# Two Mamba-style layers in one kernel: B of two states by diagonal matrices, the skip product D*u moved from TensorE to VectorE, and some smaller edits of order and layout

## The chip, the core and the metric

The kernel runs on one core of a Trainium2 chip. The metric is device time in microseconds of one execution; a kernel's time is the median of its runs. In the profile, PE is TensorE (PEld its weight loads), DVE is VectorE, ACT is ScalarE, POOL is GpSimd and SP is SyncE, which here issues nearly all DMAs. Each engine works through its own queue in order.

## The reference

The input is 8 images of 48 x 48 pixels with 192 channels. Two layers follow each other, each with a residual, each fed by a group norm. Both expand to 384 inner channels and run a selective scan with 16 states. Cut to what matters:

```python
# layer 0: four directions k of an image (rows, columns, both also backwards)
xi, z = split(einsum('bhwc,oc->bhwo', x, in_proj_w)); z = silu(z)
xi = silu(conv3x3_depthwise(xi) + conv_b)
x_dbl = einsum('bkdl,kcd->bkcl', xs, x_proj_w)          # per k: 12 dt ranks, B (16), C (16)
dt = softplus(einsum('bkrl,kdr->bkdl', dts, dt_w) + dt_bias)
h = exp(dt*A) * h + (dt*u) * B;  y = sum_n(h * C)        # the scan over 2304 pixels
y = sum of the four directions of (y + Ds*xs)
y = layernorm(y) * ln_w + ln_b
x = x + einsum('bhwd,od->bhwo', y * z, out_proj_w)
# layer 1: two stages (down the columns, then along the rows), each the sum of a forward
# and a backward Mamba over lines of 48 pixels
xs = silu(causal_conv_3taps(xs) + conv_b)
y = selective_scan(xs, dt, B, C, A) + xs * D
out = einsum('nld,cd->nlc', y * silu(z), out_proj_w)
```

## The kernel before

**Tiling.** The work is cut into items of 384 pixels: 8 lines of 48. Each layer has 192 items (layer 0: 8 images x 4 directions x 6 chunks; layer 1: 2 stages x 8 images x 6 chunks x 2 directions). The 384 channels lie as 3 blocks (`j`) of 128 partitions. An item has 16 states and so 48 segments, one for each state and block. A segment is one scan of 128 x 384 on VectorE.

**The path of one segment.** `stream` runs these as lanes:
- `decays` (L426, ACT): exp(dt*A) into a tile of the pool `a` (layer 0, 12 of them) or of `das` (layer 1, 16).
- `weighs` (L450 on POOL for the whole state, or L455 on ACT in three activations): `bT`, which is dt*u with pixels on the partitions (`dtu`, three blocks of 128 pixels x 384 channels), times B, a scalar per partition.
- `places` (L474, PE): transposes the three blocks of `bT` into a PSUM tile `b`, which gives dt*u*B with channels on the partitions. There are three such PSUM banks. State 8 alone is *direct*: B itself is transposed and VectorE multiplies by dt*u (L485).
- `scans` (L1234, L994, DVE): the scan, from `a` and `b` into `h`. Layer 0 carries the last column of `h` into the next item (L969, POOL copies it to `carry`).
- `gathers` (L509, POOL): `h` times C for the three blocks of a state; C comes broadcast by DMA as `cc` (`fetches`).
- `adds` (L526, PE): transposes `h` back and sums over the states in three PSUM banks `y`. In layer 1 nine matmuls per item with diag(D) (L538, `l_diag`) add D*u into the same banks.
- `leave` (L571): copies `y` out and transposes it back into a work bank `yb_ps`; `finish` takes it from there on VectorE (L1005, L1009 in layer 0: adds into `acc`; L1238 in layer 1: multiplies the gate `z`).

Ahead of the segments, `project` makes x_dbl of a pair of items (L295, `xd_ps`), copies it out, transposes B (`bt`) and makes dt (L338). `products` multiplies dt by u on POOL (L366) and transposes it into `dtu`. Softplus, silu and exp lie in different tables of ScalarE, so softplus and silu are done for several tiles at once and the table of exp is then put back (`tables`, L212). In layer 0, `enters` does one block of three silu thirds of `u` per image and one softplus block per pair; `prologues` computes the next image's input projection and convolution in the background; `tails` does the layer norm, the gate (silu of `z`, loaded from DRAM) and the output projection of a chunk after its fourth direction. Layer 1 has `inputs`, `gates`, `begins` and `output` for the same purposes. All work matmuls share two PSUM banks.

**The order.** The order in which the program emits instructions is the order of the queues. Each layer has a `Plan`: every step is a `Need` with a due time in segments, a cost for each engine that could do it, the steps it must come after, and whether it takes or frees a work bank. `Plan.run` simulates the engines with these costs and emits, at each point, the step that can start first, and among those ready the one due first; steps with several engines (bT on POOL or ACT, copies on ACT or DVE) go where they start first. So costs and due times set every queue's order, DMA queue included, and how bT is shared.

```python
yield Need(s + 6, {PE: 0.22}, sets=done)                  # L537: one D*u product
costs = {ACT: 0.51}; ... costs[POOL] = 2.07               # weighs: one block on ACT, a whole state on POOL
Need(need.due + 1, {DVE: 0.45}, [need], frees=need.bank, sets=[mark("gated", i, j)])   # layer 1's gate
```

Of the kernel before, what the change touches and what calls it, by code (L numbers as in the profile page):

```python
# [13 lines left out]
ALU = mybir.AluOpType  # L14
# [22 lines left out]
DIRECT = ((8,), (8,))  # L37
PE, DVE, ACT, POOL, SP = "PE", "DVE", "ACT", "POOL", "SP"
# [142 lines left out]
class Common:  # L181
# [54 lines left out]
    def diagonals(self, out, w):  # L236

        for i in range(w.shape[1]):
            self.nc.vector.tensor_scalar(out[:, i, :], self.ident, w[:, i : i + 1], None, ALU.mult)

# [38 lines left out]
    def project(self, plan, pool, p, pair, lo, mid, hi):  # L279
# [3 lines left out]

        nc, mark = self.nc, plan.mark
        tiles = {}
        dts, evacs = [], []
        for i, item in enumerate(pair):
            g, wts = 2 * p + i, item["wts"]
            at = pace(mid if i else lo, hi if i else mid, 12)
            for j in range(NJ):  # L290
                n = Need(at(), {PE: item["cost"][0]}, item["ready"] if j == 0 else (), bank=(j == 0))
                yield n
                if j == 0:
                    ps, k = self.bank(n, "xd_ps"), n.bank
                nc.tensor.matmul(  # L295
                    rows(ps[:E, :T]), wts["xp"][:, j, :], item["u"](j),
                    start=(j == 0), stop=(j == NJ - 1),
                )
# [3 lines left out]
            self.copy(got.e, xd, ps[:E, :T])  # L302
# [53 lines left out]
    def products(self, plan, pool, items, direct):  # L356

        nc, mark = self.nc, plan.mark
        last = max(n for n in range(N) if n not in direct)
        for g, item in enumerate(items):  # L360
            after = [mark("dt", g)] + ([mark("multiplied", g - 2), mark("turned", g - 2)] if g >= 2 else [])
            n = Need(g * NSEG - 20, {POOL: item["cost"][1]}, after, sets=[mark("du", g)])
# [4 lines left out]
            for b in range(TB):  # L367
                at = g * NSEG - 13 + 2 * b
# [13 lines left out]
                after = [n] + ([mark("bT", g - 2, last, b) for b in range(TB)] if g >= 2 else [])  # L382
                plan.then(Need(at + 1, COPY, after, frees=n.bank, sets=[mark("dtu", g, b)]), out)
# [9 lines left out]
    def stream(self, plan, pool, items, direct, decay, scan, finish, held, kept, weighed):  # L393
# [14 lines left out]
        states = [n for n in range(N) if n not in direct]  # L408
# [49 lines left out]

        def places():
            for s in range(total):  # L460
# [3 lines left out]
                after = [mark("bt", i)] if n in direct else [mark("bT", i, n, b) for b in range(TB)]  # L464
                if s >= 3:
                    after.append(mark("scan", s - 3))
                yield Need(s - 1.5, {PE: 0.33}, after, sets=[mark("place", s)])
                bps[s] = ps = self.ps_b.tile([P, 512], F32, tag="b", name="b")
                for b in range(TB):
                    if n in direct:  # L470
# [26 lines left out]
        def gathers():  # L497

            for f in range(total // NJ):
# [3 lines left out]
                if "carry" in item:  # L503
                    yield Need(NJ * f + 2.5, {POOL: 0.15}, after, sets=[mark("carry", i, n)])
                    item["carry"](n, hs[f])
# [5 lines left out]
        def adds():  # L511
            for s in range(total):
# [20 lines left out]
                if "diag" in item and 10 <= r < 10 + NJ * TB:  # L533

                    j, b = divmod(r - 10, TB)
                    done = [mark("skipped", i)] if r == 9 + NJ * TB else ()
                    yield Need(s + 6, {PE: 0.22}, sets=done)  # L537
                    nc.tensor.matmul(  # L538
                        item["sum"][b][:, j * P : (j + 1) * P],
                        item["own"][:, j, b * P : (b + 1) * P], item["diag"][:, j, :],  # L540
                        start=False, stop=False, skip_group_check=True,
                    )
# [33 lines left out]
        for lane in (fetches, decays, weighs, places, scans, gathers, adds):  # L576
            plan.start(lane())
        plan.start(self.products(plan, pool, items, direct))
# [3 lines left out]
def layer0(ctx, cm, x, xs, x2, w, norm):  # L582
# [36 lines left out]
    def piece(b, c, due, tag="xc", bufs=3, after=(), of=x):  # L619
# [19 lines left out]
    def weights(b, due, after):  # L639
# [8 lines left out]
        for c in range(NC):  # L648
            xc, n = yield from piece(b, c, due, after=ends[-3:-2])
# [63 lines left out]
    def gate_inputs(b, wb, ready, lo, hi):  # L713
# [3 lines left out]
        for c in range(NC):  # L717
            xc, got = yield from piece(b, c, at(), after=ends[-3:-2])
# [27 lines left out]
    def prologues():  # L746

        after = yield from first()
        for b in range(1, NIMG):
# [4 lines left out]
            for j in range(NJ):  # L754
                diag, made = yield from matrices(j, at(), conv)
                pads = []
                for c in range(NC):
                    xc, got = yield from piece(b, c, at(), after=ends[-3:-2])
# [17 lines left out]
    def first():  # L776
# [8 lines left out]
        def pads_of(c):  # L785
            nonlocal ends
            xc, got = yield from piece(0, c, -95, after=ends[-3:-2])
# [47 lines left out]

    def enters():

        for p in range(len(items) // 2):
# [3 lines left out]
            if q < 3:  # L842
# [8 lines left out]
                yield Need(lo, {ACT: 2.05 + 2 * TABLE}, after, sets=[mark("u", b, q)])  # L851
                part = slice(q * L // 3, (q + 1) * L // 3)
                nc.scalar.activation(u[:, :, part], u[:, :, part], AF.Silu)
                cm.tables()
            pair = items[g : g + 2]
            after = yield from cm.project(plan, pool, p, pair, lo, mid, hi)
            yield Need(hi, {ACT: 2 * 1.07 + 2 * TABLE}, after, sets=[mark("dt", g), mark("dt", g + 1)])
            cm.softplus(pair)
            cm.tables()

    def tails():
# [4 lines left out]
        for b in range(NIMG):  # L866
            st = None
            for c in range(NC - 1, -1, -1):
# [18 lines left out]
                n = Need(at(), {ACT: 1.06}, [n] + used)  # L887
                yield n
                sq = pool.tile([P, NJ, T], F32, tag="z", name="sq", bufs=1)
                nc.scalar.activation(sq, a, AF.Square)  # L890
                for j in range(NJ):
                    n = Need(at(), {PE: MM}, [n], bank=(j == 0))
                    yield n
                    if j == 0:
                        ps, k = cm.bank(n, "var_ps"), n.bank
# [472 lines left out]
```

## Time and profile before

| what | value |
|---|---|
| median of 3 runs | 21360.33 us (21356.79 to 21372.65) |
| the profiled execution's own time | 21367.72 us |
| its span, first to last instruction | 21366.0 us |
| granted clock of TensorE | 0.991 |
| busy: PE, DVE, ACT, POOL | 20418.5, 19769.0, 20367.7, 20007.4 us (96, 93, 95, 94% of the span) |
| weight loads (PEld) | 15817.8 us (74%) |
| DMA | 1512 MB, mean 71 GB/s |
| first scan of layer 0, last of layer 0 | 104.3 us, 10778.7 us (starts) |
| first scan of layer 1 | 10902.4 us (start) |

Busy time of an engine is the union of its instructions' lengths. Instructions of one engine overlap at their ends, so a group's busy time can hold some time in which the next one was already running; the distance from one start to the next is the finer measure of what an instruction takes from its engine. The lines are those of the kernel before.

### The profile page before, as it was taken

To read this page: it belongs to the slowest core of one execution; us is meant where nothing else is said; L and a number is where in the kernel's file an instruction comes from. 1 tells how busy PE (TensorE), PEld (TensorE's weight loads), DVE (VectorE), ACT (ScalarE), POOL (GpSimd) and SP (SyncE) were. 2 spreads that over 40 slices of the span, in tenths; PEclk is the share of its full clock that TensorE was granted. 3 is DMA by queue.
4 is the path that set the end of the run, shared out by engine and by line. 5 is a ranking of instruction groups with operands and counts; after the bars stand their busy time and mean duration, and the time that the engine had idled before them with its cause. 6 is when DMAs were issued, how large, how long until landed. Compare 5 with 4: busy or idle time off the path is not lost.

```text
span 21366.0 us, 391510 instructions
## 1 busy us (share of the span) xinstructions
PE 20418.5 (96%) x138640; PEld 15817.8 (74%) x138640; DVE 19769.0 (93%) x24601; ACT 20367.7 (95%) x38324; POOL 20007.4 (94%) x10538
## 2 busy tenths in 40 slices
PE   9989999899999999988889999999999999999999
PEld 6767777676776777766667777777777777777777
DVE  8999999999999999999979999999999999999999
ACT  8999999999999999999989999999999999999999
POOL 7999999999999999999979999999999999999999
PEclk9999999999999999999999999999999999999999
DMA  2222222222222222222222222222222222222222
GB/s 78 76 83 71 77 78 75 85 71 80 75 75 85 71 77 79 76 75 62 65 61 65 65 65 65 65 65 65 64 66 66 67 68 67 67 67 68 67 67 65
DMA packets 728904, 1512.34 MB, mean 71 GB/s; under 512 B 181508, under 2 KB 324484, under 8 KB 726824
## 3 DMA queue, kind: packets, MB, share of 16 engines
q1 hardware_dynamic: 724768, 1485.21, 23.0%
q8 instruction: 1106, 18.12, 0.4%
q14 instruction: 846, 6.93, 0.1%
q10 hardware_dynamic: 2184, 2.08, 0.0%
HBM read 1382.03 MB, written 104.99 MB: 70 GB/s over the span
## 4 chain that ended last, share of the span: by engine, by line
PE 39%; DVE 6%; ACT 4%; POOL 2%; issue 1%; DMA 0%; POOLq 0%; DVEq 0%; ACTq 0%; SPq 0%
PE b L474 12%; PE y L526 12%; DVE h L1234 3%; PE o_ps L1266 3%; PE z_ps L1171 2%; PE xi_ps L1121 2%; PE dt_ps L338 2%; PE xd_ps L295 2%; POOL h L509 2%; ACT l_da L426 1%; ACT bT L455 1%; PE y L538 1%; DVE u L1146 1%; PE du_ps L373 1%; PE yb_ps L571 1%
## 5 line engine op out<-in xcount | busy, mean ns | idle before, releaser
L509 POOL TENSOR_TENSOR h<-h,cc 128x1152 f32<-128x1152 f32 x6144 | 16158.4, 2643 | 839.7 <-DVE h L1234 205.1
L1234 DVE TENSOR_TENSOR_SCAN h<-l_da,b 128x384 f32<-128x384 f32 x9216 | 8160.5, 935 | 441.3 <-PE b L474 337.8
L474 PE MATMUL b<-ident,bT 128*128 128x128 f32 x51840 | 8022.7, 277 | 434.7 <-DVE h L994 320.8
L526 PE MATMUL y<-ident,h 128*128 128x128 f32 x55296 | 7931.6, 276 | 252.5 <-POOL h L509 235.2
L455 ACT ACTIVATE bT<-dtu,bt 128x384 f32<-128x384 f32 x14070 | 8053.2, 606 | 71.6 <-PE b L474 63.8
L474 PEld LDWEIGHTS b<-ident,bT 128*128 128x128 f32 x51840 | 6005.4, 142 | 2371.2 <-issue 721.1
L994 DVE TENSOR_TENSOR_SCAN h<-a,carry,b 128x384 f32<-128x384 f32 x7680 | 7212.0, 995 | 518.0 <-PE b L474 215.4
L526 PEld LDWEIGHTS y<-ident,h 128*128 128x128 f32 x55296 | 6363.9, 142 | 1746.7 <-POOL h L509 788.3
L426 ACT ACTIVATE a<-dt,l_A 128x384 f32<-128x384 f32 x9216 | 5206.5, 606 | 30.6 <-DVE h L994 28.2
L426 ACT ACTIVATE l_da<-dt,l_A 128x376 f32<-128x376 f32 x9216 | 5098.8, 600 | 56.6 <-DVE h L1234 53.0
L450 POOL TENSOR_TENSOR bT<-dtu,bt 128x1152 f32<-128x1152 f32 x1070 | 2264.8, 2120 | 59.0 <-PE b L474 41.5
L994 DVE TENSOR_TENSOR_SCAN h<-a,b 128x384 f32<-128x384 f32 x1536 | 1357.7, 935 | 131.2 <-PE b L474 82.5
L366 POOL TENSOR_TENSOR du<-dt,u 128x1152 f32<-128x1152 f32 x384 | 1074.8, 2799 | 166.5 <-ACT dt L354 149.1
L295 PE MATMUL xd_ps<-u,l_xp 128*44 128x384 f32 x2304 | 1143.1, 586 | 5.2 <-ACT u L1140 2.6
L338 PE MATMUL dt_ps<-xd,l_dtw 12*128 12x384 f32 x2304 | 1045.1, 535 | 0.5 <-ACT dtu L220 0.5
L738 PE MATMUL cv_ps<-pad,diag 128*128 128x384 f32 x2376 | 950.9, 489 | 1.2 <-DVE acc L1009 0.9
L1171 PE MATMUL z_ps<-xt,l_z 96*128 96x384 f32 x2304 | 922.0, 491 | 23.5 <-DVE u L1146 22.5
L1266 PE MATMUL o_ps<-z,l_out 128*96 128x384 f32 x2304 | 930.5, 486 | 0.0
L1121 PE MATMUL xi_ps<-xt,l_u 96*128 96x384 f32 x2304 | 845.5, 496 | 54.4 <-DVE u L1146 41.9
L969 POOL COPY carry<-h 128x3 f32<-128x3 f32 x2560 | 507.2, 198 | 247.4 <-DVE h L994 221.1
L1146 DVE SCALAR_TENSOR_TENSOR u<-xi_ps,l_conv_w,u 128x376 f32<-128x376 f32 (+1 forms) x1152 | 685.9, 595 | 53.0 <-ACT u L1140 27.6
L485 DVE TENSOR_TENSOR b<-b,du 128x384 f32<-128x384 f32 x1152 | 629.7, 547 | 81.2 <-PE b L474 80.9
(123 smaller groups left out, 14278.8 us busy)
## 6 DMA issues: line engine op xcount, KB each, us to landing
cc<-bc SPq DMA_DIRECT2D x3072, 384.0 KB, 3.5
xc<-in_x SPq DMA_DIRECT2D x186, 288.0 KB, 4.4
z<-v SPq DMA_DIRECT2D x144, 192.0 KB, 1.9
z<-z SPq DMA_DIRECT2D x48, 576.0 KB, 4.3
v<-v SPq DMA_DIRECT2D x126, 192.0 KB, 2.0
u<-v SPq DMA_DIRECT2D x21, 1152.0 KB, 8.0
xc<-in_xs SPq DMA_DIRECT2D x48, 288.0 KB, 3.5
x<-xc SPq DMA_DIRECT2D x48, 288.0 KB, 3.0
```

The source lines that it names most:

```text
L295: nc.tensor.matmul(rows(ps[:E, :T]), wts["xp"][:, j, :], item["u"](j), start=(j == 0), stop=(j == NJ - 1),)
L338: nc.tensor.matmul(ps[:, :T], wts["dtw"][:, j * P : (j + 1) * P], xd[:R, :], start=True, stop=True)
L426: nc.scalar.activation(dst, src, AF.Exp, scale=item["A"][:, j, n : n + 1])
L450: nc.gpsimd.tensor_tensor(to, of, by.to_broadcast((P, TB, DI)), ALU.mult)
L455: nc.scalar.activation(to[:, b, :], of[:, b, :], AF.Copy, scale=by[:, b, :])
L474: nc.tensor.transpose(ps[:, b * P : (b + 1) * P], of, self.ident)
L509: nc.gpsimd.tensor_tensor(h, h, c, ALU.mult)
L526: nc.tensor.matmul(item["sum"][b][:, j * P : (j + 1) * P], hs[f][:, j, b * P : (b + 1) * P], self.ident, is_transpose=True, skip_group_che ...
L994: nc.vector.tensor_tensor_scan(order(h[:, at % NJ, :]), order(a), order(b[:, :T]), carry[:, at : at + 1] if item["carried"] else 0.0, ALU. ...
L1171: nc.tensor.matmul(pieces(ps), wz[d][0][:, m, j * P : (j + 1) * P], lines(xts[p % 3], m, d), start=(m == 0), stop=(m == NM - 1),)
L1234: nc.vector.tensor_tensor_scan(h[:, at % NJ, :], a, b[:, :T], 0.0, ALU.mult, ALU.add)
L1266: nc.tensor.matmul(ps[:CP, :T], wout[:, 2 * stage + e, j, m * CP : (m + 1) * CP], items[2 * p + e]["z"][:, j, :], start=(e == 0 and j == 0 ...
```

## The change

For layer 0:
- **Column x products in image order.** For the two column directions, x_dbl is computed with the pixels in the order of the image (rows of 8 pixels) and turned into column order by the copy out of PSUM. The additions into `acc` for these directions run in image order as well, reading `yb_ps` at a stride.
- **1/sigma in PSUM.** The squares are made in three parts; Ln and Exp of the variance stay in the PSUM bank, and the multiplication by 1/sigma reads them there.
- **Joined table loads.** Thirds 1 and 2 of the next image's silu, and the silu of `z` for the items that have ended, are done in the softplus block of a pair (`block`). `z` has two tiles and is loaded before that block.
- **Two states by diagonal B.** States 4 and 11 get no bT. A lane `matrices` makes diag(B) for the three pixel blocks, on POOL in one instruction or on ACT in three, and `places` multiplies dtu by it: nine fp32 matmuls per state in place of nine transposes.
- Buffers: `a` has 9 tiles instead of 12, `xc` two instead of three.

For layer 1:
- **D*u by VectorE.** The nine L538 matmuls per item and `l_diag` go. `finish` adds u*D to `y` in PSUM by one `scalar_tensor_tensor` for each block, ahead of the product with the gate. `u` has six tiles instead of five and is freed at the gate.
- **The first pair sooner.** Inputs, projections and dt*u of the first pair get due times 300 segments earlier.

```diff
+DIAGONAL = ((4, 11), ())
@@ project
+            across = (lambda v: v.rearrange("p (h w) -> p h w", w=RT)) if turned else rows
-                    rows(ps[:E, :T]), wts["xp"][:, j, :], item["u"](j),
+                    across(ps[:E, :T]), wts["xp"][:, j, :], item["u"](j),
...
+                self.copy(got.e, xd.rearrange("p (w h) -> p w h", h=S),
+                    ps[:E, :T].rearrange("p (h w) -> p w h", w=RT))
@@ stream
+        def matrices():
+            for i, item in enumerate(items):
+                for n in sorted(diagonal):
+                    after = [mark("bt", i)]
+                    if placed:
+                        after += [mark("place", placed[-1] + j) for j in range(NJ)]
+                    need = Need(i * NSEG + NJ * n - 6, {POOL: 0.8, ACT: 0.72}, after, sets=[mark("matrix", i, n)])
+                    yield need
+                    to = dbs[i, n] = pool.tile([P, TB, P], F32, tag="db", name="db", bufs=1)
+                    by = item["bt"][:, :, R + n : R + n + 1]
+                    if need.e == POOL:
+                        of = self.ident.unsqueeze(1).to_broadcast((P, TB, P))
+                        nc.gpsimd.tensor_tensor(to, of, by.to_broadcast((P, TB, P)), ALU.mult)
+                    else:
+                        for b in range(TB):
+                            nc.scalar.activation(to[:, b, :], self.ident, AF.Copy, scale=by[:, b, :])
...
-                after = [mark("bt", i)] if n in direct else [mark("bT", i, n, b) for b in range(TB)]
+                if n in diagonal:
+                    after = [mark("matrix", i, n)] + [mark("dtu", i, b) for b in range(TB)]
...
-                yield Need(s - 1.5, {PE: 0.33}, after, sets=[mark("place", s)])
+                yield Need(s - 1.5, {PE: 0.67 if n in diagonal else 0.33}, after, sets=[mark("place", s)])
...
+                        nc.tensor.matmul(
+                            ps[:, b * P : (b + 1) * P], item["dtu"][:, b, j * P : (j + 1) * P],
+                            dbs[i, n][:, b, :], start=True, stop=True)
@@ adds
-                if "diag" in item and 10 <= r < 10 + NJ * TB:
-                    yield Need(s + 6, {PE: 0.22}, sets=done)
-                    nc.tensor.matmul(item["sum"][b][:, j * P : (j + 1) * P],
-                        item["own"][:, j, b * P : (b + 1) * P], item["diag"][:, j, :], ...
@@ layer0, enters
-                yield Need(lo, {ACT: 2.05 + 2 * TABLE}, after, sets=[mark("u", b, q)])
+                if q == 0 or b == 0:
+                    yield from block(lo, after, thirds=[(b, q)])
+                thirds = [(b, q + 1)] if q < 2 and b else []
+            ended = [g - 2, g - 1] if p and (g - 2) % per >= 3 * NC else []
+            for i in ended:
+                n = Need(hi - 20, {SP: 0.1}, [mark("z used", gated[-2])] if len(gated) > 1 else [], lag=DMA)
...
+                yield from block(hi, after, pair, thirds, ended)
+    def block(due, after, pair=(), thirds=(), ended=()):
+        tables = 1 + bool(pair) + bool(thirds or ended)
@@ layer0, tails
-                rs = sq[:, 0, :]
-                nc.scalar.activation(rs, ps[:, :T], AF.Ln, bias=eps)
+                rs = ps[:, :T]
+                nc.scalar.activation(rs, rs, AF.Ln, bias=eps)
                 nc.scalar.activation(rs, rs, AF.Exp, scale=-0.5)
@@ layer0
-        return pool.tile([P, T], F32, tag="a", name="a", bufs=12), lambda a, dt: (a, dt)
+        return pool.tile([P, T], F32, tag="a", name="a", bufs=9), lambda a, dt: (a, dt)
-            a, yj = seen(acc, j, k, c), rows(y)
+            a, yj = by_rows(seen(acc, j, k, c), k), by_rows(rows(y), k)
@@ layer1
+    NU = 6
+    SOON = 300
+            if p == 0:
+                lo, hi = lo - SOON, hi - SOON
-                        if i >= 5:
-                            after.append(mark("skipped", i - 5))
+                        if i >= NU:
+                            after += [mark("gated", i - NU, b) for b in range(NJ)]
@@ layer1, finish
+            nc.vector.scalar_tensor_tensor(
+                y, item["own"][:, j, :], item["D"][:, j : j + 1], y, ALU.mult, ALU.add)
             nc.vector.tensor_tensor(item["z"][:, j, :], item["z"][:, j, :], y, ALU.mult)
-        plan.then(Need(need.due + 1, {DVE: 0.45}, ...
+        plan.then(Need(need.due + 1, {DVE: 0.96}, ...
```

## The prediction

> **What bounds the kernel now.** I read the busy time by stretch first, because the two layers are separate programs with different limits: 2000 to 9000 us lies wholly in layer 0, 12000 to 20000 us in layer 1.
>
> ```profile
> core 0: us, PE busy (x) PEld busy (x) DVE busy (x) ACT busy (x) POOL busy (x), PEclk, DMA share, GB/s
> 2000.00:9000.00 7000.00, 6554.70 (x43918) 4985.44 (x43917) 6496.53 (x7659) 6692.15 (x12656) 6695.80 (x4357) 0.99 0.25 77
> 12000.00:20000.00 8000.00, 7929.34 (x55034) 6294.76 (x55032) 7525.18 (x9839) 7751.18 (x14542) 7513.42 (x2981) 1.00 0.22 66
> ```
>
> Everything is at 93% or more, so shares alone decide nothing; DMA (22 to 25%) and the clock (0.99) are out. An item has 48 decays: 6062 in the first stretch are 126.3 items of 55.4 us, 7052 in the second 146.9 items of 54.5 us. Next, the waits, for layer 0 (POOL) and then for layer 1 (POOL, DVE, PE):
>
> ```profile
> POOL carry L969 <- DVE h L994: 114.8, 124, 3.1
> POOL h L509 <- DVE h L994: 30.1, 34, 3.0
> ...
> POOL h L509 <- DVE h L1234: 152.8, 232, 3.6
> ...
> DVE h L1234 <- PE b L474: 263.2, 597, 1.5
> ...
> PE xi_ps L1121 <- DVE u L1146: 28.3, 49, 0.7
> PE z_ps L1171 <- DVE u L1146: 21.8, 35, 0.6
> ```
>
> In layer 0 all POOL waits together are 165 of 7000 us: POOL runs end to end and sets the pace, with ACT (95.6%) as its partner in making bT. In layer 1 POOL waits for about 475 us of 8000, the scans wait 263 us for PE's b, and PE's matmuls wait only 62 us in all. There PE sets the pace. Then the groups, out of the answers for the two stretches (us busy, mean ns):
>
> ```profile
> L509 POOL TENSOR_TENSOR h<-h,cc 128x1152 f32<-128x1152 f32 x2022 | 5344.6, 2648 | 172.0 <-DVE h L994 30.1 <-POOL h L509 5.2 <-POOL carry L969 0.2
> L455 ACT ACTIVATE bT<-dtu,bt 128x384 f32<-128x384 f32 x4815 | 2765.4, 606 | 24.0 <-PE b L474 21.6 <-PE y L526 0.4
> L450 POOL TENSOR_TENSOR bT<-dtu,bt 128x1152 f32<-128x1152 f32 x289 | 615.1, 2128 | 2.6 <-PE b L474 2.1 <-ACT dtu L220 0.5
> L1009 DVE TENSOR_TENSOR acc<-acc,yb_ps 128x384 f32<-128x384 f32 x288 | 210.2, 735 | 3.2 <-PE yb_ps L571 3.0
> L906 DVE TENSOR_TENSOR acc<-acc,sq 128x1152 f32<-128x1152 f32 x30 | 87.2, 2906 | 0.0
> L634 POOL TENSOR_TENSOR diag<-ident,l_conv_w 128x128 f32<-128x128 f32 x144 | 54.0, 408 | 0.0
> L1005 DVE SCALAR_TENSOR_TENSOR acc<-u,l_dsum,yb_ps 128x384 f32<-128x384 f32 x90 | 52.6, 589 | 1.4 <-PE yb_ps L571 1.3
> L884 DVE TENSOR_TENSOR acc<-acc,mu_ps 128x1152 f32<-128x1152 f32 x30 | 40.4, 1345 | 3.4 <-PE mu_ps L881 3.1
> ...
> L538 PE MATMUL y<-l_diag,u 128*128 128x128 f32 x2646 | 512.9, 276 | 0.0
> ```
>
> L455 and L450 give the split of the 15 bT states of an item: 12.7 on ACT, 2.3 on POOL. In order of time, TensorE shows what a D*u product costs it, start to start:
>
> ```profile
> 14015.36 0.39 PE L538 MATMUL y<-l_diag,u 128*128 128x128 f32 x2
> 14015.59 0.49 PE L526 MATMUL y<-ident,h 128*128 128x128 f32 x3
> 14015.91 0.49 PE L474 MATMUL b<-ident,bT 128*128 128x128 f32 x3
> ```
>
> 0.23 us for a product, 0.11 for a transpose (three in 0.33): the shown lengths (0.39, 0.49) hold a drain that the next instruction overlaps.
>
> **Layer 0, diagonal states.** Two bT states per item go. On ACT one is three activations spaced 0.51 us apart (seven decays in 3.65 us), 1.5 us; on POOL it is 2.1 us. Each gets a diag(B) instead, 128x384. POOL bounds: 0.41 us for 128 columns (L634), 2.13 for 1152 with the same broadcast (L450), so 0.83 by the line between. ACT: three of the 0.26 us of the bt copy (128x132), 0.8. I take 0.8. The planner in the kernel shares bT by its own costs (0.51, 2.07), which agree with the trace, so I count all of it on ACT and then rebalance: ACT loses 2 x (1.5 - 0.8) = 1.4 us per item. PE gains 18 products for 18 transposes: 18 x 0.12 = +2.1 us. The matrix has one buffer and its place waits for it and for all three dtu blocks; behind it in PE's queue stand adds and work matmuls. Three b banks cover about 3 us; without that cover a late matrix costs up to 0.8 us, twice per item.
>
> **Layer 0, table loads.** Silu of thirds 1 and 2, and of the gate, joins the softplus blocks. Before: 2 loads each for 24 thirds, 96 pairs, 48 gates = 336. After: 6 + 14 (first thirds) + 192 (pairs) + 30 (a third table where something joined) + 2 = 244. 92 x 1.29 us = -119 us on ACT, 0.6 per item. Squares in three parts: +0.35 us x 48, 0.1 per item. The joined block holds ACT up to 8.3 us (three tables 3.9, two softplus 2.3, silu 2.1), while decays in stock fall from 12 to 9: 9 x 1.15 = 10.4 us of scans, enough but with little over; some 30 such blocks could cost 0 to 2 us each.
>
> **Layer 0, rebalanced.** ACT falls by 1.4 + 0.6 - 0.1 = 1.9 us. Moving d states from POOL to ACT until both fall alike: 2.1 d = 1.9 - 1.5 d, d = 0.53, so both fall 1.1 us. POOL, which sets the pace, gives 1.1 to 1.15 us per item. I take 1.15: L906 at 2.9 us runs beside a busy POOL, the last one, with POOL idle, took 1.36, so POOL too should stall less. 192 x 1.15 = **-221 us** (bounds 0.4 and 1.5: -77 to -288).
>
> **Layer 0, what costs nothing or helps beside it.** Column xd products took 1.40 us start to start (3105.34 to 3106.74) against 0.77 in image order: -0.63 x 3 on half the items = -0.95 on PE, which pays half of the diagonals' 2.1. L906 with 1/sigma in PSUM should cost L884's 1.35: -1.6 us x 48 on DVE. Odd acc additions (0.85 us each in a column pass) should cost 0.53: -0.32 x 288 on DVE. Against this last speaks the Trainium skill, SBUF — State Buffer, section Door 1: PSUM has 8-byte lines and a non-contiguous PSUM pattern slows matmuls significantly; yb_ps is now read at a stride of 48 elements. The row that does that today, the 96x384 addition of o_ps (L945), takes 537 ns against 538 for a straight copy, so I take 0.53; were the rule right for DVE, this saving would be 0, and the sum the same, as DVE (92.8%) is not the pace. The z loads leave the tail: same 48 transfers of 576 KB, but issued on SP before the block, past the cc fetches, instead of waiting for L906 at the head of SP's queue. SP has room.
>
> **Layer 1, D*u.** PE loses 9 x 0.23 = 2.0 us per item; DVE gains three operations of L1005's form, 0.51 (spacing) to 0.59: 1.5 to 1.8 us, ahead of the gate product; scans queue behind it, and the work bank stays taken 0.5 us longer. The eased u buffers (six, freed at the gate) come free about when five did. Now the sum of three engines: DVE 51.2 + ACT 52.8 + POOL 51.1 = 155.1 us per item, +1.7 = 156.8, mean 52.3 if copies and bT are shared out again. At layer 0's mean use (94.7%) that gives 55.2 us, slower by 0.7; at ACT's use in layer 1 (96.9%) 54.0; if PE alone counted, 52.5. Rule against row: the Trainium skill, Perfetto Trace Analysis, Identifying the Most-Contended Engine, holds matmul occupancy a bad measure and wants weight-load occupancy, here 6295 of 8000 us, 79%. By it PE has room, ACT is the most contended, and this edit brings nothing or a loss. By the waits PE is the pace and up to 2.0 us come out. I side with the waits but let the three others stop it early: -0.55 us, 53.9. 192 x 0.55 = **-106 us** (bounds -1.3 and +0.4: -250 to +77).
>
> **Between the layers.** Last scan of layer 0 ends about 10779.7, first of layer 1 starts at 10902.41. From the first pair's normalised xt (10824.9) to that scan are 77.5 us, in which PE alternates xd and dt with z and the next pair's xi. The pair alone needs, by the same rows: xi and taps to 10841.9, silu 3.5, xd 4.3, copy and dt about 8, softplus with tables 4.8, du 2.6, dtu 0.6, bT 2.1, place 0.5: some 45 us. 32 us sooner, of which the z and xi work pushed behind it takes part back: -25. The last tail no longer waits for z and two tables (10802.1 to 10807.0): -5. Together **-30** (-5 to -50). At the start two xc buffers instead of three hold up six statistics pieces of about 3.5 us: **+5** (0 to 10).
>
> **Sum.** -221 - 106 - 30 + 5 = -352 us on the profiled execution's own 21367.7, so 21016; the runs' median lies 7 us below that execution: **21010 us**.
>
> **Rivals.**
> *Layer 1 follows PE* (14%): -2.0 x 192 = -384, with the rest 20730. For: PE's 62 us of waits. Against: ACT at 97%.
> *Layer 1 stands still* (16%): DVE, ACT and POOL keep 54.5 us; -246 us, 21115. For: their sum grows.
> *PE takes over in layer 0* (10%): in a diagonal state places and adds need 3 x (0.68 + 0.33) = 3.0 of 3.45 us, besides background matmuls; if b comes late there, layer 0 gives 60 us: 21170. Against: two states of 16, three banks.
> *D*u lands on the scan chain* (6%), the slower side: DVE's present idle time stays, and each item of layer 1 grows by the whole 1.75 us: +336 - 246 = +90, 21450. It decides from 1.5 us per item on. Against: most of that idle time is waiting for PE.
> *The plan gives it back* (4%): its new order leaves POOL as full as now and the gains elsewhere wait for it: 0 us, 21360, the unchanged time.
> My own case has 50%, its range 20880 to 21140.
>
> **How the numbers follow.** Leaving out the slower case, the unchanged one and the outer part of the first rival gives 20780 to 21230. 0.2% is 43 us, about what this measurement can tell. Faster 0.90, same 0.04, slower 0.06.
>
> **What would show it.** Right: layer 0 items near 54.3 us, POOL's bT below 2.3 per item, table loads 92 fewer, L906's successor near 1.35, column xd products at 0.8 per pair; layer 1 items near 53.9 with PE's waits grown and DVE waiting less for b; first scan of layer 1 about 90 us after the last of layer 0. Wrong: POOL waits in layer 0 grown to over 5% (PE or decays late), or DVE in layer 1 over 97% busy with items at 54.5 or more.

## The result, and the profile after

The changed kernel takes 21021.72 us (median of 4 runs, 21017.24 to 21027.79) against 21361.95 us before on the same chip: 0.984 of it, 95% interval 0.9823 to 0.9857. The profiled execution took 21021.07 us, its span is 21019.3 us, its clock 0.996. The prediction says 21010 us, 12 us from the median. That it comes so close is luck in part: layer 0 gave 48 us more than was said and layer 1 54 us less, as the scan starts in the two traces show (us; layer 0 has 192 items, layer 1 too):

| stage | before | after | difference | predicted |
|---|---|---|---|---|
| to the first scan | 104.3 | 109.0 | +4.7 | +5 |
| layer 0, first scan to last | 10674.4 | 10405.6 | -268.8 | -221 |
| last scan of layer 0 to first of layer 1 | 123.7 | 94.1 | -29.6 | -30 |
| layer 1, stage 1 | 5222.1 | 5215.9 | -6.2 | -53 |
| layer 1, stage 2 | 5219.0 | 5173.0 | -46.0 | -53 |
| after the last scan | 22.5 | 21.6 | -0.9 | 0 |

An item fell from 55.6 to 54.2 us in layer 0 and from 54.4 to 54.1 us in layer 1. The busy time of the two stretches, as shown of before:

```profile
core 0: us, PE busy (x) PEld busy (x) DVE busy (x) ACT busy (x) POOL busy (x), PEclk, DMA share, GB/s
2000.00:9000.00 7000.00, 6732.94 (x47284) 5345.49 (x47284) 6539.38 (x7802) 6703.55 (x13085) 6719.10 (x4410) 0.99 0.25 79
12000.00:20000.00 8000.00, 7828.10 (x52699) 5994.81 (x52699) 7742.41 (x10240) 7750.08 (x14599) 7640.58 (x3033) 1.00 0.22 67
```

In layer 0 POOL's share has hardly moved (95.7% to 96.0%), since the stretch holds more items (129.2, 126.3 before): per item its busy time fell from 53.0 to 52.0 us, and ACT's from 53.0 to 51.9. In layer 1 PE has gone from 99.1% to 97.9% and DVE from 94.1% to 96.8%. The waits of the changed kernel (us in total, times, longest), POOL, DVE (for both kinds of place) and ACT in layer 0, then POOL, DVE and PE in layer 1:

```profile
POOL carry L1030 <- DVE h L1059: 64.7, 75, 3.4
POOL h L548 <- DVE h L1059: 43.6, 28, 13.0
DVE h L1059 <- PE b L512: 181.2, 327, 4.5
DVE h L1059 <- PE b L503: 39.7, 76, 2.5
ACT a L435 <- DVE h L1059: 97.8, 209, 3.4
...
POOL h L548 <- DVE h L1298: 202.2, 266, 3.8
DVE h L1298 <- PE b L512: 118.3, 272, 1.3
PE b L512 <- DVE h L1298: 86.5, 304, 1.0
```

Two rows of the kernel before to set beside them, DVE in layer 0 and PE in layer 1:

```profile
DVE h L994 <- PE b L474: 172.9, 282, 3.6
...
PE b L474 <- DVE h L1234: 10.3, 46, 2.4
```

POOL still waits for almost nothing in layer 0: 1.5% at these two rows. In layer 1 the picture has turned. The scans waited 263 us for PE's transposes and now wait 118; PE waited 10.3 us for the scans to free a `b` bank and now waits 86.5. POOL waits for the scans 202 us, 50 more than before. DVE is now what the others wait for, and its own waits, all together, fell most: from 394 to 180 us, while POOL's fell from 474 to 354 and PE's rose from 62 to 153.

The granted clock of TensorE differs too (0.991 over the span before, 0.996 after), and almost all of that lies in layer 0. By the clock record of the traces, half the clock was granted for 297 us between its first and last scan before, and for 133 us after, mostly in stretches of 3.4 to 10 us. In the 3.4 us ahead of such a stretch PE was busy 46% of the time before and 56% after, against 93 and 95% on the whole, so these stretches come where PE had been waiting. What they add to the time was not separated from the waits.

The groups that the prediction's steps rest on, layer 0 and below the gap layer 1 (us busy, mean ns, then idle time before them):

```profile
L464 ACT ACTIVATE bT<-dtu,bt 128x384 f32<-128x384 f32 x4316 | 2507.7, 606 | 11.5 <-PE b L512 8.9
L459 POOL TENSOR_TENSOR bT<-dtu,bt 128x1152 f32<-128x1152 f32 x241 | 510.5, 2118 | 7.8 <-PE b L512 6.3 <-PE y L565 1.4
L483 ACT ACTIVATE db<-ident,bt 128x128 f32<-128x128 f32 x714 | 232.3, 391 | 3.2 <-PE b L503 3.0
L295 PE MATMUL xd_ps<-u,l_xp 128*44 128x384 f32 x774 | 326.3, 508 | 0.1
L1074 DVE TENSOR_TENSOR acc<-acc,yb_ps 128x384 f32<-128x384 f32 x300 | 157.3, 530 | 3.1 <-PE yb_ps L600 2.7
L971 ACT ACTIVATE acc<-acc,l_ln_b,l_ln_w 128x384 f32<-128x384 f32 x90 | 62.2, 699 | 3.5 <-DVE acc L967 3.4
L967 DVE TENSOR_TENSOR acc<-acc,var_ps 128x1152 f32<-128x1152 f32 x30 | 40.1, 1335 | 2.6 <-ACT var_ps L964 2.3
...
L1302 DVE SCALAR_TENSOR_TENSOR yb_ps<-u,l_D,yb_ps 128x384 f32<-128x384 f32 x441 | 263.7, 598 | 1.2 <-ACT l_da L435 0.8 <-ACT bT L464 0.4
```

The 7000 us hold 129.2 items: 11.1 bT states of an item on ACT and 1.87 on POOL, where it was 12.7 and 2.3. The addition L1074 takes 530 ns (735 before; both are means over straight and strided ones), the product with 1/sigma (L967) 1335 instead of 2906. One place and one matrix in order of time:

```profile
3015.80 0.83 PE L503 MATMUL b<-db,dtu 128*128 128x128 f32 x6
...
3016.47 0.49 PE L565 MATMUL y<-ident,h 128*128 128x128 f32 x3
...
3017.15 0.97 ACT L483 ACTIVATE db<-ident,bt 128x128 f32<-128x128 f32 x3
...
3017.83 0.19 POOL L1030 COPY carry<-h 128x3 f32<-128x3 f32 x1
...
3018.03 1.28 ACT L435 ACTIVATE a<-dt,l_A 128x384 f32<-128x384 f32 x2
...
3018.11 2.65 POOL L548 TENSOR_TENSOR h<-h,cc 128x1152 f32<-128x1152 f32 x1
```

Start to start, a diagonal place takes PE 0.67 us (twice a place of three transposes), the matrix takes ACT 0.88, and a carry copy takes POOL 0.28, though its own length reads 0.19. The plan of the changed kernel reckons 0.72 for that matrix and 0.15 for that copy.

### The profile page after: what moved, and what is told of

Its sections match the earlier page's. It is cut to its first block, busy times and chain, and to the rows that moved or that the text cites. A ratio compares the mean times of both kernels' runs of the same rounds, so it can differ in the third digit from the quotient of the medians.

```text
span 21019.3 us, 391720 instructions
## 1 busy us (share of the span) xinstructions
PE 20233.5 (96%) x138640; PEld 15731.1 (75%) x138640; DVE 19835.8 (94%) x25014; ACT 20092.6 (96%) x38482; POOL 19933.6 (95%) x10537
## 4 chain that ended last, share of the span: by engine, by line
PE 57%; DVE 17%; ACT 10%; POOL 9%; issue 6%; DMA 1%; DVEq 0%; POOLq 0%; SPq 0%; ACTq 0%
PE y L565 18%; PE b L512 17%; DVE h L1298 9%; POOL h L548 7%; PE dt_ps L344 4%; ACT bT L464 3%; DVE h L1059 3%; PE xd_ps L295 3%; PE cv_ps L767 3%; PE b L503 2%; PE o_ps L1333 2%; ACT l_da L435 2%; ACT a L435 2%; PE xi_ps L1190 2%; PE z_ps L1240 2%
## 5 line engine op out<-in xcount | busy, mean ns | idle before, releaser
L565 PE MATMUL y<-ident,h 128*128 128x128 f32 x55296 | 7673.2, 275 | 188.9 <-POOL h L548 175.3
L512 PE MATMUL b<-ident,bT 128*128 128x128 f32 x48384 | 7402.7, 276 | 339.2 <-DVE h L1059 162.9
L464 ACT ACTIVATE bT<-dtu,bt 128x384 f32<-128x384 f32 x13026 | 7518.3, 606 | 54.9 <-PE b L512 45.5
L565 PEld LDWEIGHTS y<-ident,h 128*128 128x128 f32 x55296 | 6273.8, 141 | 1621.5 <-POOL h L548 708.2
L512 PEld LDWEIGHTS b<-ident,bT 128*128 128x128 f32 x48384 | 5557.4, 141 | 2022.0 <-issue 629.0
L435 ACT ACTIVATE a<-dt,l_A 128x384 f32<-128x384 f32 x9216 | 5282.5, 607 | 166.3 <-DVE h L1059 152.8
L459 POOL TENSOR_TENSOR bT<-dtu,bt 128x1152 f32<-128x1152 f32 x1034 | 2188.4, 2118 | 43.8 <-PE b L512 34.0
L295 PE MATMUL xd_ps<-u,l_xp 128*44 128x384 f32 x2304 | 959.2, 505 | 21.9 <-DVE z L1305 13.9
L503 PE MATMUL b<-db,dtu 128*128 128x128 f32 x6912 | 925.1, 279 | 10.0 <-DVE h L1059 9.3
L503 PEld LDWEIGHTS b<-db,dtu 128*128 128x128 f32 x6912 | 850.7, 193 | 83.7 <-DVE h L1059 42.4
```

What stands on the lines that cost most here:

```text
L295: nc.tensor.matmul(across(ps[:E, :T]), wts["xp"][:, j, :], item["u"](j), start=(j == 0), stop=(j == NJ - 1),)
L435: nc.scalar.activation(dst, src, AF.Exp, scale=item["A"][:, j, n : n + 1])
L459: nc.gpsimd.tensor_tensor(to, of, by.to_broadcast((P, TB, DI)), ALU.mult)
L464: nc.scalar.activation(to[:, b, :], of[:, b, :], AF.Copy, scale=by[:, b, :])
L503: nc.tensor.matmul(ps[:, b * P : (b + 1) * P], item["dtu"][:, b, j * P : (j + 1) * P], dbs[i, n][:, b, :], start=True, stop=True,)
L512: nc.tensor.transpose(ps[:, b * P : (b + 1) * P], of, self.ident)
```

## The experiments

All times are medians; the changed kernel is "after" (21022). Stages are read from scan starts in each profiled execution, as above. Layer 0 of three runs below in which nothing of layer 0 was edited took 10393 to 10396 us against 10406 in after, so differences of layer 0 under about 15 us are not interpreted. Layer 1 is steadier: 10388 to 10393 us in after and the seven runs that edit nothing of it. The intervals of the ratios are about 0.0015 to each side (some 32 us), so for differences of 50 to 66 us the intervals of the two kernels still touch; what speaks for them is that the four runs of each kernel lie within 25 us, and that the kernel before took 21356 to 21363 us (medians) on the chips used.

**Layer 0: the diagonals undone.** The two states get bT again; all else stays.

```diff
-DIAGONAL = ((4, 11), ())
+DIAGONAL = ((), ())
```

> The changed kernel without the diagonal states in layer 0 (states 4 and 11 get a bT again); all else stays. The changed kernel takes 21022 us, 54.20 us per item in layer 0 and 54.11 in layer 1, from scan to scan. Theory A (POOL sets layer 0's pace, with ACT as its partner in making bT, and PE has room): ACT gains 2 x (1.5 - 0.87) = 1.3 us per item, and shared out again over ACT and POOL both rise by about 0.75 us; 192 x 0.75 = 144 us, so 21165 us. Rival B (PE is loaded by the 18 products so far that it sets the pace): PE loses 2.1 us per item, and the time stays or falls, 20950 to 21025 us.

Measured: 21132.06 us, 0.9894 (0.9877 to 0.991) of before; layer 0 10509.4, so 104 us more, 0.54 us per item, although PE's busy time per item fell from 52.1 to 51.0 us. That is nearer to the first theory than to the second. The bT split is that of before again:

```profile
L464 ACT ACTIVATE bT<-dtu,bt 128x384 f32<-128x384 f32 x4907 | 2834.0, 607 | 10.3 <-PE b L512 8.1
L459 POOL TENSOR_TENSOR bT<-dtu,bt 128x1152 f32<-128x1152 f32 x287 | 607.2, 2116 | 13.6 <-PE b L512 9.9 <-PE y L565 2.2 <-ACT a L435 1.4
```

These are 12.8 and 2.24 states per item (128.1 items in the stretch), and yet an item takes 0.8 us less than before the change: the other edits of layer 0, together, do that without the diagonals.

**Layer 0: the loads' price put back.** `tables()` is called twice for each pair's block. The second call finds the table in place and puts no load into the program: L214 has 221 loads in both traces. What comes back is the cost that the plan reckons for the block, 1.29 us for each pair.

```diff
-        cost = tables * TABLE + ...
+        cost = (tables + bool(pair)) * TABLE + ...
+        if pair:
+            cm.tables()
```

> The changed kernel with one more table load behind each of the 96 pair blocks of layer 0 (about as many as joining them took away), nothing else moved. 96 x 1.295 us = 124 us on ACT, 0.65 per item. Theory A (ACT and POOL share bT, so an ACT microsecond costs the time 0.58 of one): +72 us, 21094 us. If ACT alone set the pace: +124 us, 21146. If the loads lay beside POOL's work and cost nothing: 21022.

Measured: 21072.33 us, 0.9865 (0.9851 to 0.988), 51 us over after. So it says nothing of real loads and decides between no theories of them, but it prices a thing that had not been asked: the order that a wrong cost makes, with the same table loads, is worth 51 us here.

**Layer 0: real loads.** In every other pair block a small exp and a small silu (0.2 us each) are added, each with a table change: 96 more loads (L925 48, L214 269). Together 143 us of ACT, which the plan counts.

```diff
+        cost = ... + more * (2 * TABLE + 0.2)
...
+        if more:   # every other pair
+            nc.scalar.activation(spot[:, 1:2], spot[:, 0:1], AF.Exp)
+            nc.scalar.activation(spot[:, 1:2], spot[:, 0:1], AF.Silu)
+            cm.tables()
```

> The changed kernel with two more table loads behind every other pair block of layer 0, kept apart by an exp and a silu of one column, so that they are really made: 96 loads x 1.295 us and 96 small activations of about 0.2 us, 143 us on ACT, 0.75 per item, counted in the plan. In the earlier run with repeated loads the profile shows that none of them reached the chip (221 in that line, as without them), so its +51 us is what a cost in the plan for work that isn't there does. Theory A (ACT and POOL share: 0.58 of it): +83 us, 21105. Theory E (three engines share: a third): +48 us, 21070. ACT alone: +143 us, 21165.

Measured: 21087.98 us, 0.9871 (0.9856 to 0.9886), 66 us over after, 60 of it in layer 0: 0.46 us for each microsecond that ACT was given, midway between the two likely theories and far from ACT as the only limit.

**Layer 0: column x products at a stride again.**

```diff
-  u=lambda j, k=k, c=c: by_rows(seen(u, j, k, c), k), turned=k % 2, cost=(0.7, ...
+  u=lambda j, k=k, c=c: seen(u, j, k, c), turned=0, cost=(1.29 if k % 2 else 0.7, ...
```

> The changed kernel with x_dbl of the column directions again in column order, 1.40 us start to start per product in place of 0.77; PE gains 0.95 us per item of layer 0, 182 us over the layer. The prediction's account (PE is off layer 0's pace): nothing, 21022 us. Rival B (PE sets the pace): +182 us, 21204. A middle theory D (PE is not the pace, but a longer PE queue makes b and the work banks later, at a fifth to two fifths of its length): +35 to +75 us, 21057 to 21097.

Measured: 21080.59 us, 0.9869 (0.9854 to 0.9884), 59 us over after. Groups and waits, layer 0:

```profile
L295 PE MATMUL xd_ps<-u,l_xp 128*44 128x384 f32 x774 | 447.3, 667 | 0.0
...
DVE h L1059 <- PE b L512: 245.2, 336, 4.7
POOL carry L1030 <- DVE h L1059: 102.3, 122, 3.3
```

The mean goes from 508 to 667 ns, and what follows can be read down the chain: the scans wait for `b` 245 us instead of 181, POOL for the scans 102 instead of 65. Of the 182 us that PE got (0.63 x 3 on 96 items) a third reached the end (59 us; 47 of them in layer 0), as the last of the expectations had it. PE was not the pace of layer 0, and its time was not free.

**Layer 0: 1/sigma in SBUF again.**

```diff
-                rs = ps[:, :T]
-                nc.scalar.activation(rs, rs, AF.Ln, bias=eps)
+                rs = pool.tile([P, T], F32, tag="sq", name="rs", bufs=2)
+                nc.scalar.activation(rs, ps[:, :T], AF.Ln, bias=eps)
```

> The changed kernel with 1/sigma written to SBUF, as before, so that VectorE's product reads two SBUF tiles; the rest of the tail stays. The product goes from about 1.34 to about 2.9 us, 48 times: 75 us on DVE, 0.4 per item of layer 0. The prediction's account (costs nothing, DVE is not the pace): 21022. Theory E (DVE, ACT and POOL share work in layer 0 too, so a third of every DVE microsecond counts): +25 us, 21047. If POOL is held as well while that product runs, up to 1.5 us each of the pace-setting engine: +25 to +95 us, up to 21120.

Measured: 21080.43 us, 0.9867 (0.985 to 0.9883), 59 us over after.

```profile
L967 DVE TENSOR_TENSOR acc<-acc,rs 128x1152 f32<-128x1152 f32 x30 | 64.9, 2164 | 2.9 <-ACT rs L964 2.8
L971 ACT ACTIVATE acc<-acc,l_ln_b,l_ln_w 128x384 f32<-128x384 f32 x90 | 62.2, 699 | 17.4 <-DVE acc L967 17.3
...
L1030 POOL COPY carry<-h x2560: 176/188/1363, 110.9 to 10524.1; 128x3 f32<-128x3 f32 x197
```

48 products grew by 0.83 us, 40 us of DVE, and ACT, next in the tail, waited for them 17.3 us of the stretch instead of 3.4. POOL is held as well, as the last row shows (shortest, median and longest of the carry copies in ns; the longest is 240 in after): 18 carry copies that ran beside such a product took up to 1.36 us. Over all POOL instructions beside a product, the lengths are some 33 us more than in after. So the 59 us stand against 40 us of DVE and 33 of POOL, and of the expectations the one in which POOL is held fits; what the tail's chain (ACT, then POOL, waiting for the product) adds was not separated. The plan reckons 1.35 us for the product in both kernels.

**Layer 0: odd additions in column order again.**

```diff
-            a, yj = by_rows(seen(acc, j, k, c), k), by_rows(rows(y), k)
+            a, yj = seen(acc, j, k, c), rows(y)
...
-            Need(need.due + 1, {DVE: 0.5}, ...
+            Need(need.due + 1, {DVE: 0.75 if k % 2 else 0.5}, ...
```

> The changed kernel with the additions into acc of the column directions again in column order: 0.84 us in place of 0.53, 288 times, 89 us on DVE, 0.46 per item of layer 0. The prediction's account: nothing, 21022. Theory E (a third of every DVE microsecond counts): +30 us, 21052. DVE alone as the pace: +89 us, 21111.

Measured: 21055.58 us, 0.9856 (0.9841 to 0.9871), 34 us over after, 18 us of it in layer 0 of the profiled execution. L1074's mean goes from 530 to 731 ns, 89 us of DVE in all. The nearest expectation is the middle one, but the interval of the ratio overlaps that of after widely, so of this part only a small cost is likely, not its size.

**The kernel before with nine decay tiles.** Diagonals, real loads (96 added, where the change saved 92), column products, 1/sigma and additions cost 110 + 66 + 59 + 59 + 34 = 328 us one by one, 291 of them in layer 0 of the profiled executions; layer 0 gained 269. With some 11 us of scatter in each stage the surplus is not sure. Does the smaller stock take it? Here the kernel before gets 9 tiles in place of 12, and nothing else.

```diff
-        return pool.tile([P, T], F32, tag="a", name="a", bufs=12), lambda a, dt: (a, dt)
+        return pool.tile([P, T], F32, tag="a", name="a", bufs=9), lambda a, dt: (a, dt)
```

> The kernel before the change with 9 tiles of decays in layer 0 instead of 12, as the change has; nothing else. The parts of layer 0, each undone alone, are worth about 317 us together, the whole gained 269. If the smaller stock of decays costs the difference, this kernel takes 40 to 60 us more than the kernel before: 21400 to 21420. If the parts merely stand in for each other, the stock costs nothing: 21362 within 15 us.

Measured: 21362.13 us against 21355.95, 1.0004 (0.9995 to 1.0013). ACT now waits longer for a free tile, first the row of the kernel before, then that of this run:

```profile
ACT a L426 <- DVE h L994: 7.4, 17, 1.0
...
ACT a L426 <- DVE h L994: 74.8, 164, 1.4
```

It costs nothing that can be measured. The stock is not the cause in the kernel before; whether it is in the changed one was not tried.

**Layer 1: no D*u at all.** The product is left out, so D*u is missing from layer 1's y.

```diff
-            nc.vector.scalar_tensor_tensor(
-                y, item["own"][:, j, :], item["D"][:, j : j + 1], y, ALU.mult, ALU.add)
-  Need(need.due + 1, {DVE: 0.96}, ...
+  Need(need.due + 1, {DVE: 0.45}, ...
```

> The changed kernel without D*u in layer 1: neither TensorE nor VectorE makes it, so the output lacks that term. VectorE loses 1.5 us per item of layer 1. Theory A (in layer 1 DVE, ACT and POOL are now level and share work through copies and bT): a third of 1.5, -0.5 us per item, -96 us, 20926. Rival C (DVE alone sets the pace of layer 1): -1.5 per item, -290 us, 20732. Rival B (PE still sets it): nothing, 21022.

Measured: 20901.14 us, 0.9783 (0.9768 to 0.9797); layer 1 10276.7 us. This splits the move in two. Without D*u on either engine, layer 1 is 164 us below before: PE's 2.0 us per item, taken away with nothing put on DVE, gave 0.86. (The sixth u tile and the earlier due times are in this run too; the tile was not tried alone.) With it on DVE, layer 1 is 112 us above this run: DVE's 1.5 us per item took back 0.58. The net is the -0.27 that after shows. The first theory was the nearest, 25 us short.

```profile
12000.00:20000.00 8000.00, 7879.08 (x53306) 6078.19 (x53305) 7575.46 (x9906) 7780.29 (x14687) 7777.53 (x3097) 1.00 0.21 68
...
DVE h L1298 <- PE b L512: 228.4, 445, 1.8
```

Even then POOL, ACT and PE stand at 97.2, 97.3 and 98.5%: where DVE is eased, the other three close up at once, and the scans again wait for PE.

**Layer 1: state 8 by a diagonal.** If DVE is now the fullest, the direct state (three products of `b` with dt*u per item) is what to take from it. It gets a diagonal B, as two states of layer 0 have.

```diff
-DIRECT = ((8,), (8,))
+DIRECT = ((8,), ())
-DIAGONAL = ((4, 11), ())
+DIAGONAL = ((4, 11), (8,))
...
```

The dt*u of a later item then no longer waits for that product on VectorE.

> The changed kernel with state 8 of layer 1 by diagonal B instead of direct: per item DVE loses three products of 0.55 us = 1.65, ACT or POOL gains a matrix of 0.85, PE gains nine products for nine transposes, 1.0. Theory A (three engines level): their sum falls by 0.8, a third is 0.26 us per item, -50 us, 20972. Rival C (DVE alone sets layer 1's pace): up to -1.65 per item, -317 us, 20705. Rival B (PE sets it): +1.0 per item, +192 us, 21214.

Measured: 20961.87 us, 0.9813 (0.9798 to 0.9827), 60 us below after, 50 of them in layer 1.

```profile
12000.00:20000.00 8000.00, 7913.59 (x54295) 6202.01 (x54294) 7620.77 (x9940) 7797.02 (x14687) 7756.54 (x3163) 1.00 0.21 67
```

DVE falls from 96.8 to 95.3%, PE goes back to 98.9%, and the item is shorter. That is the first theory's number, within 10 us; PE's 1.0 us more per item did not lengthen the item.

**The change-over: not sooner.**

```diff
-    SOON = 300
+    SOON = 0
```

> The changed kernel with the due times of layer 1's first pair as they were before (no 300 segments ahead); nothing else. The record's theory: the first scan of layer 1 then comes 115 to 120 us after the last of layer 0 instead of 94, and nothing makes up for it: 21047. Rival: the work that was pushed behind the first pair (z, xi of the next pair) is paid later, so what is gained in the change-over is lost in the first items of layer 1: gap 115 to 120 but total 21022 within 8 us. Third: the due times do not bind there, gap 94, 21022.

Measured: 21032.45 us, 0.9847 (0.983 to 0.9863), 11 us over after. The time from the last scan to the first is 122.7 us instead of 94.1, so the due times do bind and alone make the 28.6 (in the other runs of the changed kernel, with these due times, this gap is 93 to 100 us). Counted from the last scan of layer 0, this run is 28.6 us behind at the first scan of layer 1, 17.6 after 14 scans, 13.8 after 96, and 21 at the last one. Neither theory is right as it stands: the gain is real, and a quarter to a half of it is given back in the first items, where the z and xi work comes that had been pushed behind the first pair. (That the whole run is only 11 us slower is in part the scatter of layer 0, which took 11 us less in it with no step edited.)

**The plan's prices.** The trace of after gives 0.27 us, start to start, for a carry copy (median; 0.28 in the lines above) and 0.88 for a matrix on ACT; with 13.3 copies an item, 0.12 each, the plan takes POOL for 1.6 us emptier than it is. No instruction is added or removed.

```diff
-  {POOL: 0.8, ACT: 0.72}     # matrix
+  {POOL: 0.83, ACT: 0.88}
-  {POOL: 0.15}               # carry
+  {POOL: 0.26}
```

> The changed kernel with two prices of its plan put at what the trace shows: a carry copy on POOL 0.26 us in place of 0.15 (13.3 per item, spaced 0.265 us), the matrix 0.88 on ACT in place of 0.72 (three activations spaced 0.29) and 0.83 on POOL in place of 0.80. No instruction is added or removed; only the order, and how bT, matrices and copies are shared between ACT and POOL, can change. Theory A (POOL still sets the pace in layer 0, 97% busy, because the plan takes it for 1.5 us per item emptier than it is): bT moves from POOL to ACT, POOL gives 0.3 to 0.7 us per item of layer 0: 20880 to 20970. Theory B (all engines are so nearly level that the prices do not matter): 21022 within 43 us. Theory C (ACT has no room; what moves to it makes the decays late): 21070 or more.

Measured: 20965.89 us, 0.9817 (0.9803 to 0.9832), 56 us below after, 48 of them in layer 0.

```profile
2000.00:9000.00 7000.00, 6743.74 (x47385) 5370.84 (x47385) 6536.87 (x7849) 6783.24 (x13250) 6628.42 (x4372) 0.99 0.25 79
...
L464 ACT ACTIVATE bT<-dtu,bt 128x384 f32<-128x384 f32 x4500 | 2609.2, 606 | 5.6 <-PE b L512 4.2
L459 POOL TENSOR_TENSOR bT<-dtu,bt 128x1152 f32<-128x1152 f32 x184 | 389.3, 2116 | 12.3 <-PE b L512 10.4 <-PE y L565 1.4 <-DVE dtu L224 0.4
```

POOL makes 1.42 bT states of an item instead of 1.87, and falls from 96.0 to 94.7% busy, with waits of 228 us instead of 141; ACT rises from 95.8 to 96.9%. That is Theory A, at the weak end of what it expected. Which of the two prices did it was not separated.

**Both.** The corrected prices and the diagonal in layer 1 together.

> The run with the plan's two prices corrected, and besides it state 8 of layer 1 by a diagonal B in place of the direct product on VectorE, which alone gave 60 us. If the two act in different layers, as Theory A has it, they add: 60 us below that run, 20820 to 20910 if the prices give what A expects; 20960 if the prices bring nothing.

Measured: 20888.08 us (20883.98 to 20889.76), 0.978 (0.9766 to 0.9795), the fastest of all kernels here: 134 us below after, 468 below before on its chip. Layer 0 is 54 us below after (48 with the prices alone), layer 1 76 (50 with the diagonal alone). So the two more than add: 134 against 56 + 60. The price of a matrix now counts in layer 1 as well, which has one per item here; that this makes the 26 us was not tried.

## Why the prediction was right, and where it was not

**Layer 0, the sum: -221 said, -269 measured.** The terms it counted were too large and those it did not count too small. The diagonals and the 92 loads were to bring nearly all of the 1.15 us per item. The relief came as it was said: busy time per item fell by 1.1 us on ACT and by 1.0 on POOL (1.1 said for both). The loads were 92 fewer, exactly (660 to 568), and ACT's three activations take 0.88 instead of 0.8. But undone alone the diagonals are worth 110 us, and 92 loads at the measured 0.46 of their time about 55: some 165 together. The step that failed is "what costs nothing or helps beside it". Column products, 1/sigma and odd additions were costed at nothing because neither PE nor DVE was the pace; undone alone they are worth 59, 59 and 34. The durations named there were right: 0.64 us saved on each column product (it is two instructions in the trace; 667 - 508 ns as the mean of all, and half of them are columns; 0.63 said), 1.335 for L967, 0.53 for L1074. That POOL should stall less beside L967 was right too, but only named and not counted: in the kernel before, POOL's instructions beside L906 were some 44 us longer in all than their usual lengths, in after 4 us beside L967. What was wrong is the model of one pace-setter with slack beside it: with four engines between 93 and 96% busy, each of these parts moved the end, and in the column run the waits of DVE and POOL grew as PE's work did.

The parts, undone one at a time, need not add up to the gain. The stock of decays is excluded as the reason, for the kernel before. The plan's order alone moves the time by about 50 us either way (the loads' price, the corrected prices), and each undone part also makes the plan order the rest anew. The granted clock moves as well: half clock for 133 us of layer 0 in after, 198 without the diagonals, 225 with 1/sigma in SBUF, but 116 with the strided column products. So the 34 to 110 us of a part cannot be divided between its own work, that order and the clock. This stays open.

**Layer 0, the split.** POOL's bT was to fall, with 0.53 states an item moved to ACT; it fell by 0.42, and by 0.87 with the plan's prices corrected. That the planner's costs "agree with the trace" was true of bT and not of the carry copy, which the prediction does not mention.

**Layer 1: -106 said, -52 measured.** The mechanism was right, the size was not: the step is "I side with the waits but let the three others stop it early: -0.55". The two ends are now known. PE's relief was worth 0.86 us, not 2.0, and DVE's load took back 0.58, which leaves 0.27 where the forecast had 0.55. The sign for it was named, scans that wait less for PE while PE waits more. Stage 1 gained 6 us and stage 2 46; without D*u it is 52 and 112, so PE's relief itself is worth less in stage 1, and the cause of that was not looked for. The Trainium skill (Perfetto Trace Analysis, Identifying the Most-Contended Engine) judges TensorE's room by its weight loads; read so, 79% leave PE room, and taking work off it brings nothing. The 164 us of the run without D*u speak against that reading. That PE alone set the pace is contradicted as well: its 2.0 us gave 0.86.

**The change-over and the start.** -30 said, -29.6 between the two scans, but the earlier due times make 28.6 of it and the tail hardly anything, not five; and a quarter to a half comes back in the first items of layer 1, which the prediction had named only as part of the 32 it reduced to 25. The start is +4.7 for +5.

**The rivals.** The slower case needed DVE's 1.5 us per item in full; 0.58 was paid. Layer 1 by itself came out halfway between the prediction's own case and the rival in which it stands still. PE taking over in layer 0: the scans wait for `b` 181 + 40 us (both place lines) where it was 173 us, and PE's price shows in the column run, but the items shortened all the same. The plan did give something back, some 50 us, through the prices of the carry copy and the matrix. The remark on PSUM in the Trainium skill (SBUF — State Buffer, Door 1) is about matmuls. The prediction asked whether it holds for VectorE, and the trace of after shows nothing of the kind: all 432 additions of L1074 took 519 to 557 ns, those of the two column directions, which read PSUM at a stride, and those of the row direction, which do not. What had cost 0.84 us in a column pass before was the addition with acc, in SBUF, at a stride.

## What to carry to other kernels

Where all engines are over 90% busy, give no edit the price zero and none its full price: where one engine alone was changed, a microsecond moved the end by 0.3 to 0.5 (PE 0.32 and 0.43, DVE 0.38 and 0.39, ACT 0.46). These rates are no sum to forecast with where work goes from one engine to another: undoing the diagonals gave ACT some 1.3 us per item and took 2.0 from PE (0.34 for each of six places). By the rates the item should have stayed or become shorter; it became 0.54 us longer. Where a planner orders the queues, compare every one of its prices with start-to-start distances in the trace, the smallest and most frequent instructions above all: a 0.15 that was 0.27, and a 0.72 that was 0.88, cost 56 us with no instruction added. Split a move between engines into its two halves by a run with the work left out.

## What was not expected of the hardware

The same fp32 product of 128x1152 on VectorE takes 1326 to 1355 ns in all 48 executions when one operand lies in PSUM, and 1334 to 3818 ns (median 2086) with both in SBUF, beside a POOL that is busy with its own SBUF products. That is a matter of where the operand lies, not of the instruction. It reaches POOL as well: a carry copy beside such a product took up to 1.36 us instead of 0.19. And that copy, left alone, keeps POOL 0.27 us from start to start although it reads as 0.19.
